# Making the 33 rows behind a unit's weights with two 64-column matmuls on half of the pixels each

## The chip, the cores and the metric

The program runs on one NeuronCore of a Trainium2 chip. The metric is the device time of one execution in microseconds (us), as a median over several. The engines are named as in the profile: PE (TensorE's matmuls), PEld (its weight loads), DVE (VectorE), ACT (ScalarE), POOL (GpSimd) and SP (SyncE, which here only issues DMAs).

## The reference, cut to what matters

Two layers follow each other on x of shape (4, 512, 64, 64) in float32. The first is self-attention over the 4096 pixels of an image with 128 inner channels; the second is a bottleneck around a 7x7 involution, a convolution whose weights are computed for each pixel. Both add their input.

```python
# layer 0, per image, xf = x as (512, 4096)
q, k, v = wq @ xf + bq, wk @ xf + bk, wv @ xf + bv          # 128 x 4096 each
attn = softmax(q.T @ k, axis=-1)                            # 4096 x 4096
x = wo @ (v @ attn.T) + bo + x
# layer 1
out = relu(s1 * (W1 @ x) + b1)                              # 128 channels
w = relu(sr * (Wr @ out) + br)                              # 32 rows
w = Ws @ w + bs                                             # 49 taps x 8 groups = 392 rows
out[c] = sum over 49 taps of w[group(c), tap] * out[c, shifted by tap]
x = s3 * (W3 @ out) + b3 + x
```

The change concerns the line with the 32 rows. A 33rd row of ones lets the next product add the bias bs.

## The kernel before, in words

**Attention.** An image's x is loaded in eight chunks of 512 pixels, each 4 x 128 channels deep. `keys_values` makes keys and values of all chunks. `attention` then goes through blocks of 512 query pixels (in the last image the last two chunks are cut into four blocks of 256, so that there are 30 blocks of 512 and 4 of 256, 34 in all). For each of 32 groups of 128 keys it issues one score matmul (`pss`, 128x512), an Exp on ACT into `pt`, one output matmul (`po`), and an addition on DVE into `pacc` that sums the denominators. Score matmuls run two steps ahead.

**Finishing a block.** `finish_block` (L448) takes a block through the softmax's division (`pl`, `rl`, `spread`, `on`), the projection `pwo` with the residual on DVE (L487), the first product of layer 1 (`p1`, named `p` in the profile, L494), and the Relu to `o1`, channels on partitions. Then `pp` (L515) transposes `o1`, ACT copies it to `o1t`, and SP writes it to a padded image `pix` in DRAM (L522). The matmul `pr` (L528, L529) makes the rows from `o1`: its stationary operand `w_slice(O_WP, 0)` has 128 columns that hold Wr twice, in columns 0 to 31 and 64 to 95; the columns beside them are zero, and the ones row comes from the Relu's bias. So `red` (L531) holds the same 33 rows on partitions 0 to 32 and again on 64 to 96, for all 512 pixels.

**Units.** A unit is four image rows, 256 pixels, held as two tiles of 128 pixels; a block of 512 holds two units. `weights` (L248) makes a unit's 392 weights per pixel, pixels on partitions: two matmuls `pw` of 33 rows each, which lie in the two halves of the array's rows (partitions 0 and 64), one per tile. `involution` (L262) then does 21 or more taps: DVE multiplies rows of `ring`, which are loaded from `pix`, by the weights (L310), and POOL adds the product to `acc` (L334). At the end POOL folds `acc` (L343), `turn_unit` transposes it (`pa`), and `close_chunk` projects (`py`), adds the residual on DVE (L386) and stores.

**The order.** Everything is recorded as one written order, with engines synchronised by semaphores. The planner that writes it keeps a clock of TensorE's work, `pe`: `mm` (L192) adds the moving columns times `PE_COLUMN`, divided by `shared`, which is 2 for `pw`. The side work is in generators: `finishing`, `closing` and `taps`; `chores` (L242) moves each by a step between the attention's matmuls. A generator that yields "wait" is held until `pe` and the planned free times of DVE, POOL and the DMAs allow it: `involution`, for instance, waits `until(free["dve"] + 0.3)` (L269) before it calls `weights`. The order therefore follows from what each matmul is charged. SP's queue is in order: x loads (L162), writes of `pix` (L522), loads of `ring` (L230, in `pump`) and stores (L392).

Of the kernel before, what the change touches and what calls it, by code (L numbers as in the profile page):

```python
# [8 lines left out]
F32 = mybir.dt.float32  # L9
# [6 lines left out]
P = 128  # L16
CT = C // P
CH = 512
# [18 lines left out]
O_WP = 6 * 512  # L37
# [13 lines left out]
UR = 4  # L51
NT = UR // 2
# [25 lines left out]
def fast_path(  # L78
# [22 lines left out]
    def pool(name, bufs, **kw):  # L101
        return ctx.enter_context(tc.tile_pool(name=name, bufs=bufs, **kw))
# [5 lines left out]
    redpool = pool("red", 3)  # L108
# [4 lines left out]
    ps = pool("ps", 2, space=bass.MemoryType.PSUM)  # L113
# [28 lines left out]
    reds, sums_c = {}, {}  # L142
# [4 lines left out]
    def until(us):  # L147
        while pe < us and not tail:
            yield "wait"

    def pe_us(us):
        nonlocal pe
        pe += us

    def takes(engine, us):
        free[engine] = max(free[engine], pe) + us
        return free[engine]
# [28 lines left out]
    def w_slice(off, t):  # L186
        return wt[:, off + t * P : off + (t + 1) * P]

    def v1(i):
        return vec[:, i : i + 1]  # L190

    def mm(o, lhsT, rhs, start=True, stop=True, shared=1):  # L192
        pe_us(rhs.free_size() * PE_COLUMN / shared)
        return nc.tensor.matmul(o, lhsT=lhsT, rhs=rhs, start=start, stop=stop)  # L194
# [18 lines left out]
    def pump():  # L213

        nonlocal load
        while load // STEP in written:
            b, row = divmod(load, STEP)
            rows, us = written[b]

            end = H + SR - UR if rows == H else rows + PAD - 1  # L220
            n = min(b * STEP + end, low + RING) - load
            n = min(n, RING - load % RING)
            if n <= 0:
                break
            for h in range(2):
                src = pix[b % 2][row + h : row + h + n, :W, :]
                windows = bass.AP(
                    tensor=src.tensor, offset=src.offset, ap=[[P, W], [WP * P, n], [1, K * P]]
                )
                nc.sync.dma_start(  # L230
                    ring[h * W : (h + 1) * W, load % RING : load % RING + n]
                    .rearrange("p r x c -> p r (x c)"),
                    windows,
                )
            free["dma"] = max(free["dma"], us)
            us = takes("dma", ROW_US * n) + LAND_US
            landing.update((load + i, us) for i in range(n))
            load += n
            if row + n == H + SR - UR:
                load = (b + 1) * STEP  # L240
# [7 lines left out]
    def weights(b, u):  # L248
        red, col = reds[b, u]
        pw = ps1.tile([P, NT, CH], F32, tag="w", name=f"pw_{b}_{u}")  # L250
        for t in range(NT):

            rows = slice(t * (P // NT), t * (P // NT) + CR + 1)
            pixels = slice(col + t * P, col + (t + 1) * P)
            mm(
                pw[:, t, : NTAP * G], red[rows, pixels], wt[rows, O_WT : O_WT + NTAP * G],
                shared=2,
            )
        return pw


    def involution():  # L262
        nonlocal low, due
        while True:
# [3 lines left out]
            acc = work2.tile([P, NT, 4, P], F32, tag="acc", name=f"acc_{b}_{u}")  # L268
            yield from until(free["dve"] + 0.3)  # L269
            pw = weights(b, u)  # L270
            begin = pe + 0.5
            accp, ops = None, []
# [175 lines left out]
    def finish_block(b, c, off, n, po, sums):  # L448

        late = b == B - 1 and c >= NCH - 2  # L450
        name = f"{b}_{c}_{off}"
        xt = xs[b, c][:, :, off : off + n]

        def pause(us, steps):
            if late:
                yield from until(us + HOP_US)
            else:
                for _ in range(steps):
                    yield

        on = work2.tile([P, CH], F32, tag="on", name=f"on_{name}")[:, :n]
        nc.scalar.copy(on, po)
        blocks = work2.tile([P, CH // TB], F32, tag="blocks", name=f"blocks_{name}")
        takes("dve", DVE_OP)
        nc.vector.tensor_reduce(
            blocks, sums.rearrange("p (k q) -> p k q", q=TB), AX.X, ALU.add, apply_transpose=True
        )
        yield from pause(free["dve"], 3)
        pl = ps.tile([P, CH // TB], F32, tag="mm", name=f"pl_{name}")[:, : n // TB]
        for i in range(CH // n):  # L470
            mm(pl, quads, blocks[:, i * n // TB : (i + 1) * n // TB], i == 0, i == CH // n - 1)
        row = (b * N + c * CH + off) // TB
        rl = rls[:, row : row + n // TB]
        nc.vector.reciprocal(rl, pl)
        spread = work1.tile([P, CH], F32, tag="rl", name=f"spread_{name}")[:, :n]
        nc.vector.transpose(
            spread.rearrange("p (k q) -> p k q", q=TB),
            rl.unsqueeze(2).broadcast_to([P, n // TB, TB]),
        )
        nc.vector.tensor_tensor(on, on, spread, ALU.mult)  # L480
        takes("dve", 0.3 + DVE_OP * n / CH)
        yield from pause(takes("dve", DVE_OP * n / CH), 5)
        for t in range(CT):
            pw = ps.tile([P, CH], F32, tag="mm", name=f"pwo_{name}_{t}")[:, :n]
            mm(pw, w_slice(O_WO, t), on)
            takes("dve", DVE_OP * n / CH)
            nc.vector.scalar_tensor_tensor(  # L487
                xt[:, t, :], pw, bo[:, t : t + 1], xt[:, t, :], ALU.add, ALU.add
            )
            for _ in range(t % 2 if late else 1 + (t != 1)):  # L490
                yield
        p1 = ps.tile([P, CH], F32, tag="mm", name=f"p1_{name}")[:, :n]
        for t in range(CT):
            mm(p1, w_slice(O_W1, t), xt[:, t, :], t == 0, t == CT - 1)  # L494
            if t == 1 and not late:
                yield
        o1 = work1.tile([P, CH], F32, tag="o1", name=f"o1_{name}")[:, :n]
        nc.scalar.activation(o1, p1, AF.Relu, bias=v1(V_B1), scale=v1(V_S1))

        def last_bias():  # L500

            for t in range(CT):
                nc.scalar.activation(xt[:, t, :], xt[:, t, :], AF.Identity, bias=v1(V_B3 + t))  # L503
                if t % 2:
                    yield

        if late:
            yield from until(pe + HOP_US)
        else:
            yield from last_bias()  # L510

        tiles = n // P
        pp = ps.tile([P, CH // P, P], F32, tag="mm", name=f"pp_{name}")[:, :tiles]
        for t in range(tiles):
            nc.tensor.transpose(pp[:, t, :], o1[:, t * P : (t + 1) * P], ident)  # L515
        pe_us(0.5)
        o1t = work1.tile([P, CH // P, P], F32, tag="o1t", name=f"o1t_{name}")[:, :tiles]
        nc.scalar.copy(o1t, pp)
        top = c * RW + off // W
        for h in range(2):  # L520
            row = PAD + top + h
            nc.sync.dma_start(  # L522
                pix[b % 2][row : row + 2 * tiles - 1 : 2, PAD : PAD + W, :]
                .rearrange("r w c -> w r c"),
                o1t[h * W : (h + 1) * W],
            )
        us = takes("dma", PIX_US) + LAND_US
        pr = ps.tile([P, CH], F32, tag="mm", name=f"pr_{name}")[:, :n]  # L528
        mm(pr, w_slice(O_WP, 0), o1)  # L529
        red = redpool.tile([P, CH], F32, tag="red", name=f"red_{name}")[:, :n]  # L530
        nc.scalar.activation(red, pr, AF.Relu, bias=v1(V_BP), scale=v1(V_SP))  # L531
        for i in range(tiles // NT):
            reds[b, top // UR + i] = red, i * NT * P

        rows = top + n // W
        written[b] = rows, us
        units.extend((b, u) for u in range(top // UR, rows // UR))
        pump()
        yield
        if late:  # L540
            yield from last_bias()


    def attention(b, kt, vT):
# [22 lines left out]
        for m, (k, j) in enumerate(steps):  # L567
# [22 lines left out]
            if j == 0:  # L590
                nc.vector.tensor_copy(paccs[k], pt)
            elif j < nj - 1:
                nc.vector.tensor_tensor(paccs[k], paccs[k], pt, ALU.add)  # L593
            else:
                sums = work1.tile([P, CH], F32, tag="sums", name=f"sums_{b}_{k}")
                nc.vector.tensor_tensor(sums, paccs.pop(k), pt, ALU.add)
                f = finish_block(b, c, off, n, pos.pop(k), sums)
                next(f)
                finishing.append(f)
# [427 lines left out]
```

## Time and profile before

| what | value |
|---|---|
| time, median of 4 runs | 2668.71 us (2666.53 to 2671.17) |
| the profiled execution's own time | 2668.24 us |
| its span, first to last instruction | 2666.4 us |
| PE busy in the span | 2632.5 us, 99% |
| DVE, POOL, ACT busy | 1864.8 us (70%), 1820.4 us (68%), 894.5 us (34%) |
| mean granted TensorE clock | 0.997 |

Each float32 matmul of the program appears as two MATMUL rows and two LDWEIGHTS rows in the trace, so that 34 `pr` matmuls are 68 rows and 128 `pw` matmuls are 256. A matmul row's duration contains an end that is modelled; what a matmul takes from the stream is the time from its start to the start of the next one. In a timeline neighbouring rows of the same kind on an engine are merged, and "x4" tells how many. 1.8 us of the profiled execution lie outside of its span.

### The profile page before, as it was taken

The numbers are of one execution on the slowest core, as the hardware profiler recorded it, in microseconds if no ns is written. First come the engines' busy times: TensorE is split into PE (matmuls) and PEld (weight loads), VectorE is DVE, ScalarE is ACT, GpSimd is POOL, SyncE is SP. The second block draws the span as 40 slices with busy tenths as digits, with TensorE's granted clock in tenths as the row PEclk, the third lists the DMA queues.
The fourth block names the chain that finished last, engine by engine and source line by source line (L and its number), as shares of the span: only waits on it lengthen the run. The fifth ranks groups of instructions, "written<-read, shape, count | busy, mean of one in ns | idle before, by whom it ended". The sixth has DMA issues, their size and how long they took to land.

```text
span 2666.4 us, 22935 instructions
## 1 busy us (share of the span) xinstructions
PE 2632.5 (99%) x6932; PEld 1232.0 (46%) x6932; DVE 1864.8 (70%) x2609; ACT 894.5 (34%) x1495; POOL 1820.4 (68%) x1194
## 2 busy tenths in 40 slices
PE   9999999999999999999999999999999999999997
PEld 4444444444444444444444444444444444446863
DVE  0347788787565777778665678778748477887887
ACT  2333333332333333333233333333323333333320
POOL 0007788788751878878774588778788077887875
PEclk9999999999999999999999999999999999999999
DMA  6032322235604233333440333333461433322532
GB/s 230 0 73 60 91 74 71 64 73 130 159 32 105 59 91 91 91 91 77 127 125 30 80 71 75 91 91 91 107 174 49 99 65 79 77 56 59 108 91 68
DMA packets 104164, 231.60 MB, mean 87 GB/s; under 512 B 5144, under 2 KB 23776, under 8 KB 103904
## 3 DMA queue, kind: packets, MB, share of 16 engines
q1 hardware_dynamic: 103888, 229.96, 35.0%
q8 instruction: 56, 0.92, 0.1%
q14 instruction: 76, 0.62, 0.1%
q10 hardware_dynamic: 144, 0.10, 0.0%
HBM read 187.28 MB, written 42.77 MB: 86 GB/s over the span
## 4 chain that ended last, share of the span: by engine, by line
PE 92%; POOL 3%; DMA 2%; DVE 2%; issue 1%; SPq 0%; ACT 0%; POOLq 0%; DVEq 0%; ACTq 0%
PE pss L194 33%; PE po L194 33%; PE p L194 4%; PE pq L194 4%; PE pwo L194 4%; PE py L194 4%; POOL acc L334 3%; PE pk L194 2%; PE pv L194 2%; PE pw L194 2%; DMA ring<-pix 1%; PE pr L194 1%; DVE prod L310 1%; PE accp L194 1%; PE pp L515 1%
## 5 line engine op out<-in xcount | busy, mean ns | idle before, releaser
L334 POOL TENSOR_TENSOR acc<-acc,prod 128x768 f32<-128x768 f32 (+3 forms) x1059 | 1693.1, 1618 | 820.4 <-DVE prod L310 561.2
L194 PE MATMUL pss<-q,k 128*128 128x512 f32 (+1 forms) x2176 | 1052.4, 570 | 0.0
L194 PE MATMUL po<-pt,v 128*128 128x512 f32 (+1 forms) x2176 | 1047.5, 568 | 0.0
L562 ACT ACTIVATE pt<-pss 128x512 f32<-128x512 f32 x1024 | 611.2, 597 | 1206.0 <-PE pss L194 1171.9
L593 DVE TENSOR_TENSOR pacc<-pacc,pt 128x512 f32<-128x512 f32 x956 | 664.3, 695 | 461.2 <-ACT pt L562 453.9
L310 DVE TENSOR_TENSOR prod<-ring,pw 128x512 f32<-128x512 f32 (+3 forms) x1092 | 898.9, 848 | 108.4 <-POOL acc L334 63.8
L194 PEld LDWEIGHTS po<-pt,v 128*128 128x128 f32 x2176 | 410.9, 190 | 469.8 <-issue 446.1
L194 PEld LDWEIGHTS pss<-q,k 128*128 128x128 f32 x2176 | 403.7, 190 | 448.2 <-issue 435.3
L386 DVE SCALAR_TENSOR_TENSOR x<-py,vec,x 128x512 f32<-128x512 f32 (+1 forms) x132 | 96.2, 730 | 59.1 <-PE py L194 57.0
L194 PE MATMUL pwo<-on,wt 128*128 128x512 f32 (+1 forms) x272 | 132.9, 576 | 3.8 <-DVE on L480 2.7
L194 PE MATMUL py<-accT,wt 128*128 128x512 f32 (+1 forms) x264 | 131.8, 583 | 1.1 <-ACT accT L371 1.0
L343 POOL TENSOR_TENSOR acc<-acc 128x512 f32<-128x512 f32 x120 | 125.4, 1045 | 9.4
L194 PE MATMUL p<-x,wt 128*128 128x512 f32 (+1 forms) x272 | 123.3, 579 | 7.3 <-DVE x L487 7.3
L503 ACT ACTIVATE x<-x,vec 128x512 f32<-128x512 f32 (+1 forms) x136 | 93.8, 694 | 95.6 <-PE p L194 91.8
L194 PE MATMUL pk<-x,wt 128*128 128x512 f32 x256 | 118.5, 602 | 5.3 <-DMA x<-x_dram 5.3
L310 DVE TENSOR_TENSOR acc<-ring,pw 128x1024 f32<-128x1024 f32 (+1 forms) x84 | 78.8, 958 | 61.2 <-PE pw L194 60.6
L194 PE MATMUL pv<-x,wt 128*128 128x512 f32 x256 | 116.8, 593 | 0.0
L194 PE MATMUL pq<-x,wt 128*128 128x512 f32 (+1 forms) x272 | 116.0, 567 | 0.0
L487 DVE SCALAR_TENSOR_TENSOR x<-pwo,bo,x 128x512 f32<-128x512 f32 (+1 forms) x136 | 96.7, 714 | 18.4 <-PE pwo L194 17.2
L194 PEld LDWEIGHTS p<-x,wt 128*128 128x128 f32 x272 | 52.1, 192 | 66.9 <-issue 54.1
L194 PEld LDWEIGHTS pwo<-on,wt 128*128 128x128 f32 x272 | 52.5, 194 | 61.8 <-issue 51.2
L194 PEld LDWEIGHTS pk<-x,wt 128*128 128x128 f32 x256 | 48.6, 193 | 64.7 <-issue 63.5
(58 smaller groups left out, 844.4 us busy)
## 6 DMA issues: line engine op xcount, KB each, us to landing
x<-x_dram SPq DMA_DIRECT2D x55, 1024.0 KB, 5.5
ring<-pix SPq DMA_DIRECT2D x30, 1344.0 KB, 15.2
ring<-pix SPq DMA_DIRECT2D x38, 896.0 KB, 13.5
out_dram<-x SPq DMA_DIRECT2D x31, 1024.0 KB, 4.2
ring<-pix SPq DMA_DIRECT2D x66, 448.0 KB, 10.2
ring<-pix SPq DMA_DIRECT2D x8, 2240.0 KB, 21.1
pix<-o1t SPq DMA_DIRECT2D x60, 128.0 KB, 2.5
ring<-pix SPq DMA_DIRECT2D x8, 224.0 KB, 3.6
```

What stands on the lines that cost most here:

```text
L194: return nc.tensor.matmul(o, lhsT=lhsT, rhs=rhs, start=start, stop=stop)
L310: nc.vector.tensor_tensor(prod[:, :, p0 : p0 + n, :].rearrange("p t d (g c) -> p t d g c", g=G), image.rearrange("p t d (g c) -> p t d g c ...
L334: nc.gpsimd.tensor_tensor(acc[:, :, d0 : d0 + n, :], acc[:, :, d0 : d0 + n, :], prod[:, :, :n, :], ALU.add,)
L343: nc.gpsimd.tensor_tensor(acc[:, :, :n, :], acc[:, :, :n, :], acc[:, :, n : 2 * n, :], ALU.add)
L386: nc.vector.scalar_tensor_tensor(xt[:, t, :], py, v1(V_S3 + t), xt[:, t, :], ALU.mult, ALU.add)
L487: nc.vector.scalar_tensor_tensor(xt[:, t, :], pw, bo[:, t : t + 1], xt[:, t, :], ALU.add, ALU.add)
L503: nc.scalar.activation(xt[:, t, :], xt[:, t, :], AF.Identity, bias=v1(V_B3 + t))
L515: nc.tensor.transpose(pp[:, t, :], o1[:, t * P : (t + 1) * P], ident)
L562: nc.scalar.activation(pt, pss, AF.Exp)
L593: nc.vector.tensor_tensor(paccs[k], paccs[k], pt, ALU.add)
```

## The change

The one matmul `pr` of 128 columns over all pixels of a block becomes two matmuls of 64 columns. The first takes the weight columns 0 to 63 and every even tile of 128 pixels and writes partitions 0 to 63; the second takes the columns 64 to 127 and every odd tile and writes partitions 64 to 127. The program gives them the array tiles of 128 rows by 64 columns at columns 0 and 64. Each is charged as `shared=2`. `pr` and `red` are half as wide (256 pixels for a block of 512, 128 for a block of 256), the Relu works on that width, and `weights` reads both halves of the rows at the same columns.

```diff
@@ weights
             rows = slice(t * (P // NT), t * (P // NT) + CR + 1)
-            pixels = slice(col + t * P, col + (t + 1) * P)
+            pixels = slice(col, col + P)
             mm(
                 pw[:, t, : NTAP * G], red[rows, pixels], wt[rows, O_WT : O_WT + NTAP * G],
                 shared=2,
@@ finish_block
         us = takes("dma", PIX_US) + LAND_US
-        pr = ps.tile([P, CH], F32, tag="mm", name=f"pr_{name}")[:, :n]
-        mm(pr, w_slice(O_WP, 0), o1)
-        red = redpool.tile([P, CH], F32, tag="red", name=f"red_{name}")[:, :n]
+
+        pr = ps.tile([P, CH // NT], F32, tag="mm", name=f"pr_{name}")[:, : n // NT]
+        for t in range(NT):
+            half = slice(t * (P // NT), (t + 1) * (P // NT))
+            mm(
+                pr[half], w_slice(O_WP, 0)[:, half],
+                o1.rearrange("p (u t x) -> p u t x", t=NT, x=P)[:, :, t, :], shared=2,
+            )
+        red = redpool.tile([P, CH // NT], F32, tag="red", name=f"red_{name}")[:, : n // NT]
         nc.scalar.activation(red, pr, AF.Relu, bias=v1(V_BP), scale=v1(V_SP))
         for i in range(tiles // NT):
-            reds[b, top // UR + i] = red, i * NT * P
+            reds[b, top // UR + i] = red, i * P
```

## The prediction

> **What bounds the kernel now.** I read the page first: busy shares, slices, and the chain that ended last.
>
> ```profile
> PE 2632.5 (99%) x6932; PEld 1232.0 (46%) x6932; DVE 1864.8 (70%) x2609; ACT 894.5 (34%) x1495; POOL 1820.4 (68%) x1194
> PE   9999999999999999999999999999999999999997
> PE 92%; POOL 3%; DMA 2%; DVE 2%; issue 1%; SPq 0%; ACT 0%; POOLq 0%; DVEq 0%; ACTq 0%
> ```
>
> PE fills every slice but the last and carries 92% of the chain. The table by stage (us, then each engine's busy time) says where that is strict: in a stretch of steady attention PE is never idle, at an image's end it loses 2.4 us in 70, and only in the tail do others bind.
>
> ```profile
> 760.00:1250.00 490.00, 489.99 (x1208) 216.54 (x1207) 361.16 (x511) 176.78 (x292) 345.56 (x223) 1.00 0.31 75
> 630.00:700.00 70.00, 67.58 (x186) 30.88 (x185) 34.61 (x39) 17.88 (x30) 54.98 (x31) 0.98 0.54 143
> 2566.00:2666.00 100.00, 81.57 (x293) 44.88 (x291) 76.27 (x101) 8.37 (x18) 60.96 (x38) 0.94 0.31 78
> ```
>
> So what `pr` takes from PE's stream counts one to one, and DVE, POOL and ACT matter only where they stop PE. Next, the timeline of one block's `pr`, with the unit's `pw` behind it, which already is a pair of matmuls in two parts of the array (start, duration, engine):
>
> ```profile
> 381.64 0.60 PE L515 MATMUL pp<-ident,o 128*128 128x128 f32 x4
> 382.07 1.02 PE L194 MATMUL pr<-o,wt 128*128 128x512 f32 x2
> ...
> 383.03 0.30 PEld L194 LDWEIGHTS pw<-wt,red 33*128 33x128 f32 x4 [0.76 <-issue]
> 383.03 0.93 PE L194 MATMUL pw<-wt,red 33*128 33x392 f32 x4
> ...
> 383.89 0.30 PEld L194 LDWEIGHTS pss<-q,k 128*128 128x128 f32 x2 [0.56 <-issue]
> 383.89 1.13 PE L194 MATMUL pss<-q,k 128*128 128x512 f32 x2
> ...
> 384.42 0.19 PEld L194 LDWEIGHTS po<-pt,v 128*128 128x128 f32 x1 [0.24 <-issue]
> 384.85 1.02 PE L194 MATMUL po<-pt,v 128*128 128x512 f32 x2
> 384.85 0.19 PEld L194 LDWEIGHTS po<-pt,v 128*128 128x128 f32 x1 [0.24 <-issue]
> ```
>
> Two things are to be seen. Undisturbed passes of 512 columns start 0.43 us apart (384.42 to 384.85), two passes to a matmul: 0.86 us, their loads hidden under the pass before. And `pw` disturbs this: `pr` to `pw` takes 0.96 us, `pw` to `pss` 0.86, `pss` to `po` 0.96.
>
> **Part 1: the price of a pair in two parts of the array, from `pw`.** Its group costs 0.10 (0.96 less `pr`'s own 0.86) + 0.86 + 0.10 (0.96 less `pss`'s 0.86) = 1.06 us. A pass of 392 columns is 0.427 x 392/512 = 0.327 us, so four passes in turn would take 1.31, two rounds of two at a time 0.65. The passes do run two at a time, and 0.40 us is the price of going into this mode and out of it: the array is left to run empty twice, and the first load behind each switch is in the open, where in the plain stream it is hidden. `pw`'s group looks like this wherever nothing else delays it, 64 times.
>
> **Part 2: `pr` before.** 30 blocks at 0.858 us and 4 of 256 columns at 0.43.
>
> **Part 3: `pr` after, the pair running together.** Two rounds of 256 columns are 2 x 0.2135 = 0.427 us. To this comes the switch. Its one part that depends on the shape is the pair's own load in the open: 64 columns instead of 128. The groups of loads give the slope:
>
> ```profile
> L194 PEld LDWEIGHTS pw<-wt,red 33*128 33x128 f32 x256 | 19.3, 184 | 39.5 <-issue 24.8 <-DVE prod L310 4.9 <-ACT red L531 3.4
> L194 PEld LDWEIGHTS pr<-o,wt 128*128 128x128 f32 x68 | 10.3, 191 | 0.0
> L627 PEld LDWEIGHTS pn<-ones,okr 128*1 128x1 f32 x2 | 0.1, 80 | 0.5 <-DVE x L386 0.5
> ```
>
> One column takes 80 ns, 128 take 191, 33 rows or 128 make little difference; so 64 columns take 0.055 us less, and the switch 0.345 us. A block of 512 becomes 0.427 + 0.345 = 0.77 us, 0.085 less than now; a block of 256 becomes 0.2135 + 0.345 = 0.56, 0.13 more. The trace shows no pair side by side in columns, so the load is bounded: if it is no shorter, or the second half's load follows the first's, 0.40 us again (gain 0.03, loss 0.185). I take the shorter, since the four loads of `pw` stand in 0.30 us and so run beside each other. Sum: 30 x -0.085 + 4 x 0.13 = -2.0 us (bound: -0.9 + 0.74 = -0.2).
>
> **Part 4: neighbours in the written order.** In the new order 31 pairs stand between plain matmuls, and three (the last block of images 0 to 2) directly before a `pw`: one way out of a mode, with its load, falls away, 3 x -0.20 = -0.6 us. Four `pw` that stood one matmul behind their `pr` now stand two behind, so that they no longer wait for `red`; the first stood 1.03 us behind the start of a `pss` (169.31 to 170.34) instead of 0.96: 4 x -0.08 = -0.3 us. The Relu falls from 777 ns to 563 (its rows at 512 and 256 pixels), 30 times, on ACT at 34%: nothing, as only those four `pw` waited for it; PE's stream covers it. PSUM and DMA traffic do not grow.
>
> **Part 5: what the planner moves.** The clock `pe` is charged 0.43 us less per block (13.8 in all) where the stream saves 0.085, so side work is written later against it. The new order is the old one with small steps: `pw` of units 0, 4, 5 and 11 of each image stand one or two matmuls later, some `pa` and `py` one step later; POOL's order is the same, and after the last attention there are the same 70 tap products. PE waits for none of it in the steady stretches. Two covers need naming. The load of each image's last x chunk moves on SP's queue behind two `pix` writes: issued at 380.05 us before, it comes behind 382.89 + 1.26, so 4.1 later, lands 5.5 us on (the median of such loads) at 389.7, and its first reader starts at 396.2. And unit 11 starts 1.72 us later, just ahead of the image's end, where PE does wait:
>
> ```profile
> PE p L194 <- DVE x L487: 7.3, 3, 2.4
> 604.42 14.79 POOL L334 TENSOR_TENSOR acc<-acc,prod 128x512 f32<-128x512 f32 x12 [6.27 <-DVE prod L310]
> 624.87 13.47 POOL L334 TENSOR_TENSOR acc<-acc,prod 128x768 f32<-128x768 f32 x7 [5.66 <-DVE prod L310]
> ```
>
> POOL is backlogged from 624.87 on, and DVE's residual stands behind its taps; but the later start falls in the first half of the unit, ahead of an idle 5.66 us. DVE's order from there to the wait is unchanged, and so I cost the move at nothing; if that cover failed, see rival 3.
>
> **Sum.** -2.0 - 0.6 - 0.3 = -2.9 us, with the bound -1.1. The profiled execution took 2668.24 us, 0.5 under the median; against the median, 2668.7 - 2.9 = 2665.8 us.
>
> **A rule against the change.** In the trace a load of all 128 rows (384.42) runs while the pass before it, on the same 128 rows, is in flight. The Trainium skill, page "TensorE: Matmul & The Clock Gate", part 3, "What overlaps and what doesn't", says that loads overlap with running matmuls only when the row group differs, and two column halves have all rows in common. The trace disagrees for whole-array matmuls and cannot speak for halves; by the rule the pair would take turns, rival 1. The same part's table gives 2.38 for three column tiles; an estimate at that efficiency (0.79) makes the two rounds 0.54 us and the sum about +0.6.
>
> **Rivals.**
> 1. *The halves take turns.* Both halves need all 128 partitions of `o1` at once, which `pw`'s never do: each reads its own 64. If the array takes one such stream at a time, four passes remain and the switch comes on top: 30 x 0.427 + 4 x 0.2135 = +13.7, sum +10.8, 2679.5 us. For it: no row shows such a pair. Against it: the array did run two `pw` at a time. It eats the gain from 0.10 us more a block (2.9/30) and shows from 0.27 (8.2/30).
> 2. *Three rounds*: the second pass of one half runs with the first of the other only: +6.8, 2672.6 us. Against it: `pw`'s four passes took two rounds.
> 3. *The pair runs, but the image's end gets worse*: unit 11's 1.72 us reach the residual at three image ends, and each longer stop brings PE's clock down for a window (the row of the stage 630 to 700 has 0.98): about 3 x (1.7 + 1.7) = +10, 2676 us. Against it: the idle 5.66 us.
> 4. *The switch is free between column halves*: all 0.40 us fall away, the pair costs 0.427: -13.8, 2655 us. Against it: all 64 `pw` groups paid.
>
> **How the numbers follow.** Chances: forecast 0.50, rival 1 0.28, rival 2 0.06, rival 3 0.05, rival 4 0.11. 0.2% is 5.3 us, about what a measurement of this kernel can tell from no change. Faster: rival 4, 0.11. Slower: rivals 1 and 3, 0.33. Same: 0.56. The forecast's own range is 2664 to 2668; the range given reaches over rival 1, with 1.5 us for the spread of runs, to 2681, and leaves out rival 4: 2663 to 2681.
>
> **What would show it.** In the timeline of a block after: `pp` to `pr`, `pr` to the next matmul, and that one's own length, 0.77 us in all beyond `pss`'s and `pp`'s plain times if right; about 1.20 if the halves take turns, 0.98 for three rounds, 0.43 if switches are free. The loads of `pr` should have a mean near 135 ns. The wait of `p` for x should stay near 7.3 us in three times; more, and rival 3 has come. The forecast is wrong if the pair's passes do not start side by side.

## The result, and the profile after

The changed kernel takes 2664.8 us in the median of 40 runs (2659.93 to 2669.17) against 2668.49 us of 60 runs of the kernel before: a ratio of 0.9986 with a 95% interval of 0.9981 to 0.9990, or 2.7 to 5.1 us less. The forecast was 2.9 us less, 2665.8 us.

First the page of the changed kernel, the same rows as before: PE still fills the span and carries the chain, and 68 matmul rows have come in.

```profile
span 2661.1 us, 23096 instructions
PE 2627.5 (99%) x7000; PEld 1226.2 (46%) x7000; DVE 1866.5 (70%) x2609; ACT 888.3 (33%) x1495; POOL 1822.9 (69%) x1194
PE 91%; POOL 3%; DMA 3%; DVE 2%; issue 1%; SPq 0%; ACT 0%; POOLq 0%; DVEq 0%; ACTq 0%
```

Then the timeline of the changed kernel around the `pr` of the same block as was shown of before (start, duration, engine, line and operation):

```profile
381.18 0.60 PE L515 MATMUL pp<-ident,o 128*128 128x128 f32 x4
...
381.71 0.20 PEld L194 LDWEIGHTS pr<-o,wt 128*64 128x64 f32 x4 [0.17 <-issue]
381.71 0.65 PE L194 MATMUL pr<-o,wt 128*64 128x256 f32 x4
...
382.29 0.30 PEld L194 LDWEIGHTS pss<-q,k 128*128 128x128 f32 x2 [0.39 <-issue]
382.30 1.12 PE L194 MATMUL pss<-q,k 128*128 128x512 f32 x2
...
383.26 1.02 PE L194 MATMUL po<-pt,v 128*128 128x512 f32 x2
```

`pr` to `pss` now takes 0.58 us in place of 0.86, but `pp` to `pr` takes 0.53 (0.44 before) and `pss` to `po` 0.96 (0.86 undisturbed). In nanoseconds of the trace's starts the four passes begin at 0, 7, 267 and 273: the halves do run side by side, in two rounds of 0.213 us with a load of 0.053 in the open ahead of the first, and the next matmul starts at 583. (The split of 267 into 53 and 213 comes from the pairs of 256 pixels, whose second passes begin at 160: 128 columns more take 0.107 us.) With 0.094 on the way in and 0.104 on the way out, 0.78 us in all stand against 0.86 before; between blocks with nothing else changed the gain is 0.080 us. All 30 pairs of 512 pixels begin like this, and 27 of them end like this; the other three stand directly before a `pw` and have no way out of their own. Pairs of 256 pixels cost 0.57 us instead of 0.43.

The loads, from the groups of before and after:

```profile
L194 PEld LDWEIGHTS pr<-o,wt 128*64 128x64 f32 x136 | 6.7, 134 | 5.7 <-issue 5.7
```

134 ns for 64 columns, 191 for 128 before: the shorter load that the prediction took.

To see where the rest of the 2661.1 us moved, the span is divided by the trace's starts of matmuls into **steady stretches** (from the queries of an image's second block to the first key matmul of the next image, and in the last image to the queries of its second block of 256), **image ends** (the three pieces between), and the **tail** (the rest of the last image, up to the last matmul). The same division serves all runs below (us, from one profiled execution each; medians and ratios are from the timed runs):

| run | median | ratio to before, 95% interval | steady | ends | tail |
|---|---|---|---|---|---|
| before | 2668.49 | | 1932.85 | 389.1 | 220.8 |
| changed | 2664.8 | 0.9986 (0.9981 to 0.9990) | 1930.03 | 387.3 | 221.5 |
| old charge | 2664.24 | 0.9981 (0.9972 to 0.9990) | 1928.27 | 393.6 | 220.8 |
| old matmul, new charge | 2667.98 | 0.9994 (0.9985 to 1.0003) | 1932.91 | 388.7 | 221.2 |
| first half twice | 2676.3 | 1.0028 (1.0017 to 1.0039) | 1940.71 | 389.9 | 221.7 |
| four quarters | 2660.71 | 0.9969 (0.9957 to 0.9981) | 1924.14 | 391.6 | 220.6 |
| pairs beside weights | 2656.14 | 0.9953 (0.9940 to 0.9967) | 1925.31 | 390.8 | 217.6 |
| changed, unit 11 4 us later | 2657.53 | 0.9963 (0.9949 to 0.9977) | 1930.04 | 381.6 | 221.3 |
| changed, unit 11 10 us later | 2680.13 | 1.0039 (1.0026 to 1.0053) | 1930.70 | 403.5 | 222.0 |
| pairs beside weights and unit 11 4 us later | 2648.7 | 0.9922 (0.9908 to 0.9935) | 1925.31 | 383.1 | 217.7 |
| before, unit 11 4 us later | 2663.39 | 0.9979 (0.9970 to 0.9988) | 1932.84 | 383.5 | 222.1 |

In four of these kernels more of the time lies outside of the span than the 1.8 us of the others: 2.5 us in most executions of the old charge, 2.5 to 3.6 in those of the old matmul with the new charge, 2.0 to 3.2 with the pairs beside the weights, 2.8 to 3.8 in the kernel before with unit 11 later. Why is not shown; differences of a microsecond between the medians of these are therefore not read as the stream's.

In the steady stretches PE never stops, and two runs of the same stream agree to 0.01 us (1930.03 and 1930.04; 1925.31 twice). There the change is worth 2.82 us. The ends scatter by some microseconds between profiled executions: PE stops at each for 2.4 us, and behind the stop the clock is at half rate for a window of 3.4 us at some of them, at two of three ends in the profile of before and at one of three after. The rows by stage show it by the granted clock (the third column from the end), here the first and the third end of the changed kernel; the first had 0.98 before:

```profile
630.00:700.00 70.00, 67.57 (x192) 31.14 (x191) 35.43 (x41) 17.99 (x31) 56.62 (x32) 1.00 0.58 152
1922.00:1992.00 70.00, 67.55 (x190) 30.86 (x189) 34.27 (x41) 18.50 (x31) 55.58 (x34) 0.98 0.61 159
```

So of the 5.3 us by which the two spans differ, 2.8 are the steady stretches. The ends give 1.8: the three pairs there stand directly before a `pw` and save 0.28 us each (from `pp` to the matmul behind `pw` 1.97 us instead of 2.25), 0.8 in all, and the other 1.0 is within the scatter of the ends. Behind the last matmul, where the last store lands, another 1.3 are gone, and the tail is 0.7 longer; neither is shown to come from the change.

### The profile page after: what moved, and what is told of

It reads as the page before. It is cut to its first block, busy times and chain, and to the rows that moved or that the text cites. A ratio compares the mean times of both kernels' runs of the same rounds, so it can differ in the third digit from the quotient of the medians.

```text
span 2661.1 us, 23096 instructions
## 1 busy us (share of the span) xinstructions
PE 2627.5 (99%) x7000; PEld 1226.2 (46%) x7000; DVE 1866.5 (70%) x2609; ACT 888.3 (33%) x1495; POOL 1822.9 (69%) x1194
## 4 chain that ended last, share of the span: by engine, by line
PE 91%; POOL 3%; DMA 3%; DVE 2%; issue 1%; SPq 0%; ACT 0%; POOLq 0%; DVEq 0%; ACTq 0%
PE pss L194 34%; PE po L194 33%; PE p L194 4%; PE py L194 4%; PE pwo L194 4%; PE pq L194 4%; POOL acc L334 3%; PE pk L194 2%; PE pw L194 2%; DMA ring<-pix 2%; PE pv L194 2%; DVE prod L310 1%; PE accp L194 1%; PE pr L194 1%; PE pp L515 0%
```

## The experiments

**1. The old charge.** The pairs as they are, the planner charged as before.

```diff
-                o1.rearrange("p (u t x) -> p u t x", t=NT, x=P)[:, :, t, :], shared=2,
+                o1.rearrange("p (u t x) -> p u t x", t=NT, x=P)[:, :, t, :],
```

> The two column halves as in the changed kernel, but each charged at its full 256 columns, so that the planner's clock advances by 0.43 + 0.43 us per block as before and the side work stands where it stood (10 instead of 3 pairs directly before a pw). Theory (the gain is the array's): the pair still takes 0.78 us with both of its ways in and out; the seven more neighbours each save one way out, 0.20 us, so about 1.4 us faster than the changed kernel, 2663.4, less 0.3 for the four pw that wait for red again: 2663.7 us. Rival (the gain comes from the side work that moved): the time goes back to the one before, 2668.5 us.

Measured: 2664.24 us; the steady stretches are 1.76 us shorter than the changed kernel's. Seven more neighbours at 0.198 us (0.104 of a way out and 0.094 of a way in) are 1.39; four `pw` that again stand behind a short `pl` bring 0.38 (below); and the 0.3 us of waiting for `red` that was expected back did not come, since the narrower `red` is ready in time. The sum, 1.77, leaves nothing over. In the median of the times only 0.6 us of it shows, in the median of the spans 1.25 (2661.7 against 2662.95), as 2.5 us lie outside of the span in most of its executions. Its profile is of the slowest of the eleven, 2666.4 us: one image end was 5 us longer there, with 2.5 us of waiting in front of a `pw` and 6.8 us at half rate behind it. The gain comes with the pairs and not with the planner's charge, which moves most of the side work.

**2. The old matmul with the new charge.**

```diff
-        mm(pr, w_slice(O_WP, 0), o1)
+        mm(pr, w_slice(O_WP, 0), o1, shared=2)
```

> The one matmul of 128 columns as before, but charged at half, so that the side work is written as in the changed kernel. Theory: four waits of pw for red fall away (-0.3 us), four pw that stood behind a short pl now stand behind a full po (+0.4 us): no change, 2668.5 us within 0.7. Rival (the moved order makes the gain): near the changed kernel's 2664.8 us.

Measured: 2667.98 us, ratio 0.9994 with 1 inside the interval, and 0.06 us more in the steady stretches (-0.32 + 0.38 = +0.06). What the charge moves is worth nothing by itself, as the theory had it.

**3. The first half twice.**

```diff
+            if t == 0:
+                nc.tensor.matmul(
+                    pr[half], lhsT=w_slice(O_WP, 0)[:, half],
+                    rhs=o1.rearrange("p (u t x) -> p u t x", t=NT, x=P)[:, :, t, :],
+                    start=True, stop=True,
+                )
```

> The first half's matmul is issued twice, before the second half's; the order of the side work is nearly the changed kernel's. Two matmuls on the same 64 columns can't run together. Theory: two more passes of 0.2135 us per block of 512 on one half take turns, 30 x 0.43 + 4 x 0.21 = +13.7 us over the changed kernel, 2678.5 us, what rival 1 of the prediction would have cost; less if the second half's passes fill in. Rival: if passes on other columns only seemed to run together, the four passes of the changed kernel would take turns as well and six would cost half as much again, +7 us.

The timeline of one block, with the extra matmul as L537:

```profile
309.93 0.60 PE L515 MATMUL pp<-ident,o 128*128 128x128 f32 x4
310.46 0.66 PE L194 MATMUL pr<-o,wt 128*64 128x256 f32 x4
310.94 0.59 PE L537 MATMUL pr<-o,wt 128*64 128x256 f32 x2
311.47 1.13 PE L194 MATMUL pss<-q,k 128*128 128x512 f32 x2
312.43 1.02 PE L194 MATMUL po<-pt,v 128*128 128x512 f32 x2
```

`pr` to `pss` is 1.01 us against 0.58: 0.425 more, two passes of 0.213. Passes on the same 64 columns take turns, passes on different ones don't, and the written order doesn't matter: the second half's matmul stands last in the kernel's text, but both its passes run beside the first two, and the extra ones come after. The trace doesn't show the order in which the matmuls were queued; that the second half starts 13 ns behind the first and not 7 fits a queue with the extra matmul in between. The steady stretches grow by 10.7 us: 26 pairs at 0.425 are 11.05, and in eight of these blocks a `pa` stands directly behind the pair, which makes the way out 0.05 shorter. The time is 11.5 us over the changed kernel's, 2 less than the 13.7 expected; the rest of the difference lies in the ends and the tail, where the scatter is of the same size. This is the price that rival 1 would have had.

**4. Four quarters.** Four tiles of 32 columns, a quarter of the pixels each; the ones row and the pixels' right places are left out.

```diff
+        for t in range(4):
+            part = slice(t * TB, (t + 1) * TB)
+            pe_us(n // 4 * PE_COLUMN / 2)
+            nc.tensor.matmul(
+                pr[part], lhsT=w_slice(O_WP, 0)[:, part], rhs=o1[:, t * (n // 4) : (t + 1) * (n // 4)],
...
+        for t in range(2):
+            nc.scalar.activation(
+                red[:, t * (n // 4) : (t + 1) * (n // 4)], pr, AF.Relu, bias=v1(V_BP), scale=v1(V_SP)
+            )
```

> Four matmuls of 32 columns on a quarter of the pixels each, charged as in the changed kernel; the ones row and the pixels' places are left out (each part has 32 rows, and the Relu copies the quarters twice), so this tells time alone. Theory (rounds shrink, the switch stays): two rounds of 128 columns, 0.2135 us instead of 0.427, and a load of 32 columns, 0.03 us shorter: 0.54 us a block against 0.78, 30 x -0.24 + 4 x -0.13 = -7.7 us against the changed kernel, 2657 us. Rival (the price of a switch grows with the number of parts, or four streams of the same 128 partitions can't be fed): no gain or a loss, 2664 us and more.

Its timeline and its loads:

```profile
309.89 0.60 PE L515 MATMUL pp<-ident,o 128*128 128x128 f32 x4
310.42 0.43 PE L533 MATMUL pr<-o,wt 128*32 128x128 f32 x8
310.78 1.12 PE L194 MATMUL pss<-q,k 128*128 128x512 f32 x2
311.74 1.02 PE L194 MATMUL po<-pt,v 128*128 128x512 f32 x2
```
```profile
L533 PEld LDWEIGHTS pr<-o,wt 128*32 128x32 f32 x272 | 5.4, 108 | 5.7 <-issue 5.7
```

`pp` to `pr` is 0.53 and `pss` to `po` 0.96 again, `pr` to `pss` 0.36: 0.227 us less a block where 0.24 was expected, 5.9 us over the steady stretches. Loads of 128, 64, 32 and 1 columns take 191, 134, 108 and 80 ns, close to a straight line. So what the switch costs doesn't grow with the number of parts but for the 7 ns by which each next part starts later, and four streams of the same 128 partitions are fed at full rate: second passes begin 133 ns behind the first, 0.107 us of 128 columns and 0.027 of load. The median, 2660.71, is 3.7 short of that theory's 2657; the ends were 4.3 us longer here than in the changed kernel's profile.

**5. The pairs beside the weights.** The old charge, and the pair held for up to three steps of its generator, a unit's `pw` held while a pair is near:

```diff
+            while soon and not pending and not tail:
+                yield "wait"
+            if pending:
+                pending.pop()()
             pw = weights(b, u)
...
+        if not late:
+            pending.append(make_rows)
+            for _ in range(3):
+                if make_rows in pending:
+                    yield
```

`make_rows` holds the lines of `pr` and `red`; `soon` is set ahead of `last_bias` and cleared by `make_rows`.

> Old charge as in the run before, and in addition the pair of a block is held for up to three steps, and a unit's pw is held while a pair is near, so that 26 of the 34 pairs stand directly before a pw (10 with the old charge alone, 3 in the changed kernel). Theory (a way out of a mode and its load, 0.20 us, falls away with each neighbour, the side work hides the delay): 16 x 0.20 = 3.2 us less than the old charge alone in the steady stretches, 5.0 less than the changed kernel: about 2660 us. Rival (delaying units costs what the neighbours save): 2664 us or more.

The timeline of one block of it:

```profile
381.59 0.65 PE L195 MATMUL pr<-o,wt 128*64 128x256 f32 x4
382.17 0.93 PE L195 MATMUL pw<-wt,red 33*128 33x392 f32 x4
383.03 1.13 PE L195 MATMUL pss<-q,k 128*128 128x512 f32 x2
383.99 1.02 PE L195 MATMUL po<-pt,v 128*128 128x512 f32 x2
```

From columns in two to rows in two directly: `pr` to `pw` is 0.58, as `pr` to `pss` was, and `pw`'s own way in is gone. The steady stretches are 4.72 us shorter than the changed kernel's and 2.96 shorter than the old charge's, 15 neighbours at 0.198. The kernel is faster than expected, 2656.14 us; the tail is 3.9 us shorter than the changed kernel's, which the theory doesn't contain and whose cause stays open.

**6. Unit 11 later.** The prediction named a cover: POOL's idle time ahead of the second half of unit 11. In the changed kernel it has shrunk from 5.66 to 3.95 us, by the later start, and PE's waits for the residual at the ends are what they were:

```profile
605.26 14.78 POOL L334 TENSOR_TENSOR acc<-acc,prod 128x512 f32<-128x512 f32 x12 [8.07 <-DVE prod L310]
623.99 13.48 POOL L334 TENSOR_TENSOR acc<-acc,prod 128x768 f32<-128x768 f32 x7 [3.95 <-DVE prod L310]
```
```profile
PE p L194 <- DVE x L487: 7.3, 3, 2.5
```

Two runs move the unit further, the second with 10 in place of 4:

```diff
             yield from until(free["dve"] + 0.3)
+            if u == 11 and b < B - 1:
+                yield from until(pe + 4)
             pw = weights(b, u)
```

> The changed kernel, with unit 11 of images 0 to 2 held for 4 us more of the planner's clock before its weights. In the changed kernel POOL is idle for 3.95 us ahead of that unit's second half, so a later start of up to that much should be covered. Theory: the stops at the image ends (7.3 us in three) don't grow by more than a microsecond in all; but the planner also writes two of the residuals ahead of taps they stood behind, so they may shrink. Rival 3 of the prediction (the start reaches the residual): 3 x 4 us and the clock's half rate on top, +12 us and more.

> The same with 10 us, more than the cover. In the written order all four residuals of the image's last block now stand ahead of unit 12's sixth tap product on DVE (behind the twelfth in the changed kernel), while POOL's backlog is 6 us longer. Theory (the stop is the residual's place behind taps that wait for POOL, not the unit's start): the stops of p for x shrink from 7.3 us to about 0, and with them the half-rate windows: 5 to 10 us faster than the changed kernel if units 12 and 13 being late costs nothing further on. Rival (the unit's start sets the stop): 3 x 6 us longer, 2680 us.

With 4 us: 2657.53 us, 7 us faster than the changed kernel. The wait of `p` for the residual is gone; PE's waits in that run are

```profile
PE pk L194 <- DMA x<-x_dram: 6.4, 2, 4.9
PE pvt L404 <- ACT vs L435: 2.9, 4, 0.7
PE accp L194 <- DVE prod L312: 2.9, 6, 1.2
PE pwo L194 <- DVE on L482: 2.4, 1, 2.4
```

and there is no half-rate window left at an image's end. The last of the block's four residuals now stands on DVE ahead of three tap products that it used to stand behind. In the changed kernel it came after the sixth product of 128x768, each of which waits for POOL:

```profile
658.19 0.95 DVE L310 TENSOR_TENSOR prod<-ring,pw 128x768 f32<-128x768 f32 x1 [0.93 <-POOL acc L334]
659.06 0.75 DVE L487 SCALAR_TENSOR_TENSOR x<-pwo,bo,x 128x512 f32<-128x512 f32 x1
```

With 4 us it comes after the third, though unit 11 is later:

```profile
655.35 0.95 DVE L312 TENSOR_TENSOR prod<-ring,pw 128x768 f32<-128x768 f32 x1 [1.48 <-POOL acc L336]
656.22 0.74 DVE L489 SCALAR_TENSOR_TENSOR x<-pwo,bo,x 128x512 f32<-128x512 f32 x1
```

POOL's second half of the unit follows the first without idle time there. With 10 us the same wait is gone too, and yet the kernel takes 2680.13 us:

```profile
PE pr L194 <- DVE x L388: 9.0, 3, 3.0
PE pw L194 <- DVE prod L312: 8.0, 3, 2.7
```

Later consumers wait in its place: a `pr` behind the other residual, and the `pw` of a later unit, three times each, with half-rate windows behind both. So the stop was the residual's place behind taps that wait for POOL, as the theory had it; but of the "if" in that expectation, units 12 and 13 being late costs nothing, the run showed the opposite, 15 us over the changed kernel. A start that is not covered does cost the image's end, as rival 3 had it, though by other waits than that of `p`; the point where it begins lies between 4 and 10 us.

**7. Both together, and unit 11 without the change.** The first is experiment 5 with the 4 us of experiment 6, the pair that goes before unit 11's weights held for up to eight steps; the second is the kernel before with the two lines of experiment 6.

> The pairs beside the weights and unit 11 held for 4 us, with the pair of the block before it held along; 26 of 34 pairs stand before a pw, and the residuals at the image ends stand as in the run that held unit 11 for 4 us. Theory (the two gains are separate: the stream's switches in the steady stretches, the stops at the ends): steady stretches 1925 us as with the pairs beside the weights, image ends 382 as with unit 11 held, so about 8 us faster than the pairs beside the weights: 2648 to 2651 us. Rival (they are the same microseconds): no faster than 2656 us.

> The kernel before, its one matmul of 128 columns and all, with unit 11 held for 4 us more. Theory (the stops at the image ends have nothing to do with the column halves): the stops of p for x, 7.3 us, and the half-rate windows behind them go here too, 6 to 9 us faster than before: 2660 to 2663 us, with the steady stretches at 1932.9. Rival (it works only with the changed kernel's order): 2668 us.

Measured: 2648.7 us for both (ratio 0.9922, 16 us faster than the changed kernel), with steady stretches of 1925.31 and ends of 383.1 us, the two gains side by side. On the kernel before, 2663.39 us, 5 us faster than it was, with its steady stretches unmoved at 1932.84: what is gained at the image ends owes nothing to the column halves. The waits of `p` are gone there too, but not every half-rate window: the granted clock at the second image end was 0.98 in its profile, behind waits of 0.7 us of `pvt` and 1.4 of `pk`.

## Why the prediction was right, point by point

- **PE's stream is the bound, and what leaves it counts one to one.** Right: the steady stretches, where PE never waits, account for each edit to some hundredths of a microsecond.
- **Part 1 and 3, the price of a pair from `pw`.** Right in kind and size. A block of 512 went to 0.78 us (0.77 forecast), a gain of 0.080 (0.085); a block of 256 lost 0.14 (0.13). The load took 134 ns, where the slope between `pn` and `pr` gives 136, and the halves' loads run beside each other.
- **Part 4, neighbours.** The three pairs directly before a `pw` cost what was said: `pr` to `pw` 0.58, no second way in. The four waits for `red` are gone, 0.08 each. Two terms of the same sort were missed. In eight blocks a `pa` had stood directly behind `pr` and started 0.07 us late, with 0.03 more between its two transposes; it stands behind a `pss` now: -0.78. It does so with either charge (in experiment 1 too) and not with the old matmul (experiment 2), so this move came with the pairs and not with the planner's clock; how is not shown. Part 5 speaks of moves of `pa` and sets them at nothing. And four `pw` had stood behind a `pl` of 16 columns, which is too short to hide the next load anyway; now they stand behind a full `po`, so that this load is paid twice: +0.38. In the steady stretches, 26 blocks: 26 x -0.080 - 0.32 - 0.78 + 0.38 = -2.80, measured -2.82; by the prediction's own terms it would have been -2.5. With the three pairs at the image ends, 3 x -0.28 = -0.84, and those in the tail, -0.08 + 4 x 0.14 = +0.48, the measured gaps give -3.2 us in all. That the forecast of -2.9 lies so near is in part luck: the two missed terms have opposite signs and half cancel.
- **Part 5, the planner.** Right for what the charge moves: it was worth +0.06 us in the steady stretches of experiment 2, PE's stops at the image ends stayed at 7.3 us in three, and POOL's idle time shrank by 1.71 us, the later start.
- **Rival 1, turns**, is refuted by the starts at 0, 7, 267 and 273 ns and by experiment 3, which shows what turns look like. **Rival 2**, three rounds, falls with the same starts. **Rival 4**, a free switch: 0.094 and 0.104 us were paid around each pair between plain matmuls, and 0.156 more within it (0.583 against two rounds of 0.213). **Rival 3** did not come, and experiment 6 shows its cover.
- **The rule weighed against the change.** Second-half loads began 7 ns behind the first's, on the same rows, and the second passes' loads 53 ns on, while the first passes were in flight. By the rule of the Trainium skill, page "TensorE: Matmul & The Clock Gate", part 3, "What overlaps and what doesn't", they should have waited; the measurement decides against it for column halves. That part's 2.38 for three column tiles, taken as an efficiency, would have made rounds of 0.27 us; they were 0.213, as for whole-array passes (the 0.267 from the first pass to the second hold the load of 0.053).

What is left between the 2.9 us of the forecast and the 3.7 of the medians is inside the interval, 2.7 to 5.1.

## What to carry to other kernels

Splitting a matmul in two over the array buys half of its columns' time, but pays a fixed price for going into the mode and out of it, here about 0.35 us in a stream where everything else is hidden; read that price from a pair that the kernel already has, and put pairs of any split side by side so that they share it. A planner's charge can be wrong by five times the gain and cost nothing while its moves stay inside idle time, so name that idle time and its length. And a gain larger than the change's own was none of the array's, 5.7 us at the image ends: three stops of 2.4 us in which one engine's queue held a needed result behind work that waited for a third.

## What the runs showed of the hardware that was not expected

- Matmuls of two parts of the array don't need to be written side by side: with a repeated first half written in between, the other half's two passes still ran beside the first two, 13 ns later instead of 7.
- Going from columns in two to rows in two costs no more than going to the whole array does: `pr` to `pw` is 0.58 us, as `pr` to `pss` is, and `pw`'s own way in, 0.094 us, falls away.
- A stop of PE of 2.4 us was followed by a half-rate window of 3.4 us at some image ends and not at others of one execution: at the first two of three in the profile of before, at the third alone in that of the changed kernel. The mean granted clock of the changed kernel's executions goes from 0.994 to 0.998.
